# Attention with layer norms and a sign FFN: a step's scores and maxima issued in two rounds of two heads

## The chip, the cores and the metric

The kernel runs on one core of a Trainium2 chip. The metric is the device time of one execution in microseconds (us). Before the change three timed runs gave 4376.77, 4377.27 and 4377.44 us; the median is 4377.27.

The engines are called as the profile calls them: PE is TensorE (PEld its weight loads), ACT is ScalarE, DVE is VectorE, POOL is GpSimd, SP is SyncE. PSUM is the memory that PE writes its results to: eight banks, each 128 partitions by 512 f32 values here.

## The reference

Input x is 4 x 2048 x 512 in f32. There are 16 heads of 32 columns.

```
q, k, v = x @ Wq.T, x @ Wk.T, x @ Wv.T          # split into 16 heads of 32
attn    = softmax(q k^T / sqrt(32)) v            # per batch and head, over 2048 keys
x       = layernorm(x + attn)
w       = +1 or -1 by the sign of the FFN weights
y       = clip((x @ w.T) * scale + bias, -100, 100)
out     = layernorm(x + y)
```

## The kernel before

**Groups, query blocks, steps.** The work is cut into 16 groups n: four batches by four sets of four heads. A group's queries come in four blocks of 512 (qb), its keys in 16 chunks of 128 (kc). One step s is one chunk of keys against one block of queries for the four heads of a group: 64 steps a group, 1024 steps in all. Heads of 32 columns fill a quarter of PE's rows, so head h uses the row strip h (partitions 32h to 32h + 31) and four heads can stand side by side.

**Scores (L325 to L344).** The scores of a step are transposed: 128 keys on the partitions, 512 queries in the columns, one PSUM bank for each head. The softmax needs the row maximum subtracted, so each bank gets two matmuls: at L329 ones times `negm` (the negated maxima, split into three bf16 parts that sum to the f32 value) starts the accumulation, and at L335 key times query in f32 is added. Four bf16 matmuls are issued, then four f32 ones. ACT then takes the exponential of each bank (L342) into `p`, which has five buffers.

**Maxima (L266 to L303).** Before a block's scores can start, its maxima must be known. They are found by a second score matmul in the other orientation (queries on the partitions), 22 steps ahead: `units(s)` says which units of maxima step s computes. One unit is 128 queries against 512 keys for four heads: four f32 matmuls (L277) into four banks. DVE finds the maxima of the first three heads from PSUM (L284). The fourth bank is copied by ACT to a tile `moved` in SBUF (L296), and the function `later` has DVE search that tile near the end of the step. `max_parts` (L305) joins a block's parts, splits them into bf16 and issues the transposing DMA that makes `negm`; in one step of each block it stands between the first and the second maximum on DVE.

**The rest of a step.** In the order of issue (loop at L843): scores, maxima, then "fillers" that a planner (L770) has chosen, such as projections for the next group (`piece`, L235), transposes, FFN thirds or denominators. In every even step follows `weighted` (L346): the probabilities of the two steps before times v, on column strips, into one bank, which DVE adds to an SBUF tile (L365). Then `later`, and `add_up` (L374): POOL adds `p` to the running sum of the block (L379), 14 of 16 steps in a block.

**What sets the order.** The schedule is manual: each engine executes in the order of issue. Which PSUM bank is used is decided at build time by `take` (L82): it picks the bank that a small clock model (`runs`, `spend`, `give`) thinks is free first. The model decides nothing but the bank. On the chip a matmul waits by semaphore until its bank has been read.

```
def give(i, engine, us):
    free_at[i] = spend(engine, us, clock["PE"] + 0.2) + 0.1
```

Of the kernel before, what the change touches and what calls it, by code (L numbers as in the profile page):

```python
# [11 lines left out]
F32 = mybir.dt.float32  # L12
BF16 = mybir.dt.bfloat16
AF = mybir.ActivationFunctionType
ALU = mybir.AluOpType
AX = mybir.AxisListType
# [4 lines left out]
def kernel(  # L21
# [11 lines left out]
    nc = tc.nc  # L33
    B, S, D = x.shape
    P = 128
    H = 16
    HD = D // H
    HG = 4
    NG = H // HG
    DC = D // P  # L40
    QB = 512
    NQB = S // QB
    NTQ = QB // P
    NT = S // P
    NKB = S // QB
    EPS = 1e-5
    MAX_VAL = 100.0
    SM_SCALE = 1.0 / math.sqrt(HD)
    STEPS = NQB * NT
# [7 lines left out]
    const = ctx.enter_context(tc.tile_pool(name="const", bufs=1))  # L57
    xpool = ctx.enter_context(tc.tile_pool(name="xpool", bufs=2))
    stage = ctx.enter_context(tc.tile_pool(name="stage", bufs=2))
    mpool = ctx.enter_context(tc.tile_pool(name="mpool", bufs=2))  # L60
    cpool = ctx.enter_context(tc.tile_pool(name="cpool", bufs=1))
    dram = ctx.enter_context(tc.tile_pool(name="dram", bufs=1, space=bass.MemoryType.DRAM))
    xtpool = ctx.enter_context(tc.tile_pool(name="xtpool", bufs=NQB))
# [3 lines left out]
    ppool = ctx.enter_context(tc.tile_pool(name="ppool", bufs=5))  # L67
# [3 lines left out]
    small = ctx.enter_context(tc.tile_pool(name="small", bufs=2))  # L71
# [5 lines left out]
    ps = psum.tile([P, 8, QB], F32, name="ps")  # L77
    clock = {"PE": 0.0, "ACT": 0.0, "DVE": 0.0}
# [3 lines left out]
    def take():  # L82
        i = min(range(8), key=lambda k: free_at[k])
        clock["PE"] = max(clock["PE"], free_at[i])
        free_at[i] = math.inf
        return i

    def runs(shape, us):

        clock["PE"] += us + (0.1 if form[0] != shape else 0.0)  # L90
        form[0] = shape

    def spend(engine, us, ready=0.0):
        clock[engine] = max(clock[engine], ready) + us
        return clock[engine]

    def give(i, engine, us):

        free_at[i] = spend(engine, us, clock["PE"] + 0.2) + 0.1

    def cols_of(i, a, b):
        return ps[:, i, : a * b].rearrange("p (a b) -> p a b", a=a)
# [4 lines left out]
    ones_bf = const.tile([P, P], BF16, name="ones_bf")  # L107
# [81 lines left out]
    xc = {}  # L189
    kT = {}  # L190
    qT = {}
    vv = {}
    negm = {}
    parts = {}
# [68 lines left out]
        piece(tokens(n, t), weights("wv", n), vv[n][:, t, :], P)  # L263


    def max_unit(n, qb, u, between):  # L266

        qc, kb = divmod(u, NKB)
        if u == 0:
            parts[n, qb] = small.tile([P, NTQ, HG, NKB], F32, tag="part", name="part")  # L270
        part = parts[n, qb]
        if n == qb == 0:
            kb, qc = divmod(u, NTQ)
        banks = [take() for _ in range(HG)]
        for h in range(HG):
            rows = slice(h * HD, (h + 1) * HD)
            nc.tensor.matmul(  # L277
                ps[:, banks[h], :], lhsT=qT[n, qb][rows, ts(qc, P)],
                rhs=kT[n][rows, ts(kb, QB)], start=True, stop=True,
            )  # L280
        runs("rows", 0.86)

        def row_max(h, src):
            nc.vector.tensor_reduce(  # L284
                part[:, qc, h : h + 1, kb], src, AX.X, ALU.max, negate=True
            )

        for h in range(HG - 1):
            row_max(h, ps[:, banks[h], :])
            give(banks[h], "DVE", 0.6)  # L290
            if h == 0 and between is not None:
                max_parts(*between, banks[h])
                give(banks[h], "DVE", 1.25)

        moved = mpool.tile([P, QB], F32, tag="moved", name="moved")
        nc.scalar.copy(moved, ps[:, banks[-1], :])  # L296
        give(banks[-1], "ACT", 0.6)

        def later():
            row_max(HG - 1, moved)  # L300
            spend("DVE", 0.6, clock["ACT"])

        return later  # L303

    def max_parts(n, qb, i):  # L305
        part = parts.pop((n, qb))
        nm = cols_of(i, NTQ, HG)
        sp = split[qb % 2]
        nc.vector.tensor_reduce(nm, part, AX.X, ALU.min)
        nc.vector.tensor_copy(sp[:, :, :, 0], nm)  # L310
        nc.vector.tensor_tensor(nm, nm, sp[:, :, :, 0], ALU.subtract)
        nc.vector.tensor_copy(sp[:, :, :, 1], nm)
        nc.vector.tensor_tensor(sp[:, :, :, 2], nm, sp[:, :, :, 1], ALU.subtract)
        negm[n, qb] = small.tile([P, QB], BF16, tag="negm", name="negm")
        nc.sync.dma_start_transpose(
            out=negm[n, qb].rearrange("p (t q) -> p t q", t=NTQ),
            in_=sp.rearrange("p t h d -> p (t h d)"),
        )
# [3 lines left out]
    def is_last(n, qb):  # L322
        return n == B * NG - 1 and qb == NQB - 1

    def scores(n, qb, kc):  # L325
        banks = [take() for _ in range(HG)]
        for h in range(HG):
            rows = slice(h * HD, (h + 1) * HD)
            nc.tensor.matmul(  # L329
                ps[:, banks[h], :], lhsT=ones_bf[rows, :], rhs=negm[n, qb][rows, :],  # L330
                start=True, stop=False,
            )
        for h in range(HG):
            rows = slice(h * HD, (h + 1) * HD)
            nc.tensor.matmul(  # L335
                ps[:, banks[h], :], lhsT=kT[n][rows, ts(kc, P)], rhs=qT[n, qb][rows, :],
                start=False, stop=True,
            )
        runs("rows", 1.08)
        p = ppool.tile([P, HG, QB], F32, tag="p", name="p")  # L340
        for h in range(HG):
            nc.scalar.activation(p[:, h, :], ps[:, banks[h], :], AF.Exp, scale=SM_SCALE)  # L342
            give(banks[h], "ACT", 0.49)
        return p  # L344

    def weighted(pair):  # L346
# [36 lines left out]
    def ones_times(b, p, start, stop):  # L383
        for h in range(HG):
            nc.tensor.matmul(  # L385
                ps[h * HD : (h + 1) * HD, b, :], lhsT=ones, rhs=p[:, h, :],
                start=start, stop=stop,
            )
        runs("cols", 0.86)
# [12 lines left out]
    def denominators(n, qb):  # L402

        if is_last(n, qb):
            b = sums[0]
        else:
            b = take()
            for k, p in enumerate(last_p.pop((n, qb))):
                ones_times(b, p, k == 0, False)
            whole = acc.pop((n, qb))  # L410
            ones_times(b, whole, False, True)
        if is_last(n, qb):
            dT = mpool.tile([P, QB], F32, tag="moved", name="dT")
        else:
            dT = whole[:, 0, :]
        nc.scalar.copy(dT, ps[:, b, :])
        give(b, "ACT", 0.6)
        acc[n, qb] = dT
        if not is_last(n, qb):
            columns_of_sums(n, qb)  # L420
            at(step[0] + 2, reciprocals, n, qb)
# [184 lines left out]
    ahead = {}  # L606
# [3 lines left out]
    def at(step, f, *args):  # L610
        behind[step].append(lambda: f(*args))
# [78 lines left out]
    start = -LEAD0 - 5  # L690
# [66 lines left out]
    def units(s):  # L757

        def first(s):
            return min(max(s + min(LEAD0 + max(s, 0) // 2, LEAD), 0), total)  # L760

        return range(first(s), first(s + 1))
# [74 lines left out]
    _, used = plan()  # L837
    chosen, _ = plan(used)
    held = []
    before = None  # L840
    s = start
    step = [start]
    while s <= max(*chosen, *behind):  # L843
        step[0] = s
        now = None
        if 0 <= s < total:
            n, at_n = divmod(s, STEPS)
            qb, kc = divmod(at_n, NT)
            now = (n, qb, kc, scores(n, qb, kc))
        fillers = chosen[s]  # L850
        if s < 0:
            for t in fillers:
                t[3](*t[4])
        later, more = None, list(units(s))
        if more:
            n, at_n = divmod(more.pop(0), STEPS)
            later = max_unit(n, *divmod(at_n, NT), ahead.get(s))
        elif s in ahead:
            i = take()
            max_parts(*ahead[s], i)  # L860
            give(i, "DVE", 1.25)
        if s == total:
            weighted(held)
            held = []
        if s >= 0:
            for t in fillers:
                t[3](*t[4])
        if s % 2 == 0 and held:
            weighted(held)
            held = []  # L870
        if later is not None:
            later()
        for u in more:
            n, at_n = divmod(u, STEPS)
            max_unit(n, *divmod(at_n, NT), None)()
        if now is not None:
            add_up(*now, before)
            before = now[3]
            held.append(now)
        for f in behind[s]:  # L880
            f()
        s += 1
# [36 lines left out]
```

## Time and profile before

| | before |
|---|---|
| median of three runs | 4377.27 us |
| span of the profiled execution | 4375.3 us, about 2 us below the timed runs |
| first score matmul starts | 70.5 us |
| last add on POOL ends | 4302.6 us |
| PE clock granted | 0.997 of full |
| ACT exponentials (L342) | 4096 x 602 ns, 2114.8 us busy |
| DVE weighted sums (L365) | 448 x 692 ns |
| POOL running sums (L379) | 889 adds of about 4.54 us |
| DMA | 101.4 MB, mean 23 GB/s |

The span is from the first to the last instruction of one profiled execution. A group line of the profile has line, engine, operation, output and inputs, shape and count; behind the bar stand the busy time in us, the mean of one in ns, and the idle time just ahead of them with what ended most of it. An f32 matmul appears as two rows, each with its weight load, so four heads make eight rows. In a timeline each line has start, length, engine, line, operation and count. Lengths of PE rows are modelled and contain some time of the pipeline, so starts are compared.

### The profile page before, as it was taken

How to read it: one execution, taken by the hardware profiler on the slowest of the kernel's cores; microseconds unless marked ns; L12 is line 12 of the kernel's file. 1: busy time of each engine (PE TensorE's matmuls, PEld its weight loads, DVE VectorE, ACT ScalarE, POOL GpSimd, SP SyncE). 2: the span in 40 equal slices, each digit the busy share in tenths (PEclk: the TensorE clock that was granted, in tenths of full speed). 3: DMA queues.
4: the chain of work that ended last, by engine and by line, in shares of the span. 5: the costliest groups of instructions: out<-in, count | busy, mean ns of one | idle time of the engine just before them, and what ended most of it. 6: DMA issues, size and time to landing. Idle time of an engine off the chain costs nothing.

```text
span 4375.3 us, 89213 instructions
## 1 busy us (share of the span) xinstructions
PE 4340.7 (99%) x36092; PEld 2136.2 (49%) x36092; DVE 3316.3 (76%) x5908; ACT 2998.5 (69%) x6173; POOL 4082.7 (93%) x940
## 2 busy tenths in 40 slices
PE   9999999999999999999999999999999999999998
PEld 5444444454454554445445454455545544455443
DVE  6777777777777777777777777777777777777774
ACT  4666666676667667676676766767667676767665
POOL 4999999999999999999999999999999999999993
PEclk9999999999999999999999999999999999999999
DMA  2000000010001000011000100001100000001101
GB/s 72 11 13 17 11 21 10 16 40 18 21 13 29 11 23 20 11 45 36 21 20 11 33 10 21 23 10 50 28 20 21 20 21 23 20 11 33 24 23 49
DMA packets 260326, 101.40 MB, mean 23 GB/s; under 512 B 169420, under 2 KB 234956, under 8 KB 259912
## 3 DMA queue, kind: packets, MB, share of 16 engines
q1 hardware_dynamic: 258952, 93.86, 8.9%
q8 instruction: 282, 4.62, 0.4%
q10 hardware_dynamic: 960, 1.84, 0.1%
q14 instruction: 132, 1.08, 0.1%
HBM read 54.26 MB, written 33.02 MB: 20 GB/s over the span
## 4 chain that ended last, share of the span: by engine, by line
PE 95%; POOL 2%; ACT 1%; DVE 1%; issue 0%; DMA 0%; ACTq 0%; POOLq 0%; DVEq 0%; SPq 0%
PE ps L353 21%; PE ps L277 20%; PE ps L335 20%; PE ps L235 16%; PE ps L329 8%; PE ps L568 5%; PE ps L385 3%; POOL acc L379 2%; PE ps L427 1%; PE ps L223 1%; PE ps L554 1%; ACT p L342 1%; DVE part L284 1%; ACT xg_last L544 0%; PE ps L135 0%
## 5 line engine op out<-in xcount | busy, mean ns | idle before, releaser
L379 POOL TENSOR_TENSOR acc<-acc,p 128x2048 f32<-128x2048 f32 x825 | 3743.3, 4537 | 102.6 <-ACT p L342 42.4
L342 ACT ACTIVATE p<-ps 128x512 f32<-128x512 f32 x4096 | 2114.8, 602 | 1130.9 <-PE ps L335 1124.8
L284 DVE TENSOR_REDUCE part<-ps 128x1 f32<-128x512 f32 x3072 | 1934.0, 683 | 771.2 <-PE ps L277 770.8
L277 PE MATMUL ps<-kT,qT 32*128 32x512 f32 x8192 | 1112.2, 590 | 0.1
L335 PE MATMUL ps<-qT,kT 32*128 32x512 f32 x8192 | 1075.8, 592 | 0.0
L353 PE MATMUL ps<-p,vv 128*32 128x512 f32 x8192 | 983.4, 598 | 0.2 <-ACT p L342 0.2
L277 PEld LDWEIGHTS ps<-kT,qT 32*128 32x128 f32 x8192 | 541.4, 185 | 379.5 <-issue 189.4
L284 DVE TENSOR_REDUCE part<-moved 128x1 f32<-128x512 f32 x1024 | 692.4, 676 | 0.5 <-ACT moved L296 0.4
L296 ACT COPY moved<-ps 128x512 f32<-128x512 f32 x1024 | 631.1, 616 | 20.2 <-PE ps L277 19.6
L353 PEld LDWEIGHTS ps<-p,vv 128*32 128x32 f32 x8192 | 220.1, 109 | 685.7 <-issue 345.1
L329 PE MATMUL ps<-negm,ones_bf 32*128 32x512 bf16 x4096 | 442.5, 385 | 8.6 <-DMA negm<-split 3.9
L335 PEld LDWEIGHTS ps<-qT,kT 32*128 32x128 f32 x8192 | 407.4, 185 | 44.4 <-issue 27.4
L379 POOL TENSOR_TENSOR acc<-p 128x2048 f32<-128x2048 f32 x64 | 290.8, 4544 | 103.9 <-ACT p L342 103.9
L365 DVE TENSOR_TENSOR oT<-ps,oT 128x512 f32<-128x512 f32 x448 | 309.8, 692 | 94.3 <-PE ps L353 57.7
L329 PEld LDWEIGHTS <-ones_bf 32*128 32x128 bf16 x4096 | 105.8, 91 | 554.9 <-issue 521.6
L235 PEld LDWEIGHTS ps<-wvT,xT 128*128 128x128 f32 x2048 | 251.1, 191 | 79.6 <-ACT p L342 74.0
L235 PE MATMUL ps<-wvT,xT 128*128 128x128 f32 x2048 | 279.3, 280 | 0.3 <-ACT p L342 0.2
L235 PE MATMUL ps<-xT,wqT 128*128 128x256 f32 x1024 | 250.2, 387 | 0.0
L235 PE MATMUL ps<-xT,wkT 128*128 128x256 f32 x1024 | 249.1, 387 | 0.0
L235 PEld LDWEIGHTS ps<-xT,wkT 128*128 128x128 f32 x1024 | 184.8, 189 | 65.4 <-ACT p L342 43.2
L235 PEld LDWEIGHTS ps<-xT,wqT 128*128 128x128 f32 x1024 | 184.3, 189 | 61.9 <-ACT p L342 41.0
L568 PEld LDWEIGHTS ps<-wsT,nT 128*128 128x128 f32 x1152 | 167.8, 189 | 94.3 <-ACT p L342 93.3
(75 smaller groups left out, 1720.3 us busy)
## 6 DMA issues: line engine op xcount, KB each, us to landing
xc<-in_L_attn_x_dram SPq DMA_DIRECT2D x60, 256.0 KB
res<-xc SPq DMA_DIRECT2D x60, 256.0 KB
xs<-in_L_attn_x_dram SPq DMA_DIRECT2D x48, 256.0 KB
xg<-res SPq DMA_DIRECT2D x12, 1024.0 KB
out_dram<-xg SPq DMA_DIRECT2D x12, 1024.0 KB
first_x<-in_L_attn_x_dram SPq DMA_DIRECT2D x16, 256.0 KB
xg_last<-res SPq DMA_DIRECT2D x4, 768.0 KB
out_dram<-xg_last SPq DMA_DIRECT2D x3, 1024.0 KB
```

The lines of the kernel that those rows point to most:

```text
L235: nc.tensor.matmul(pp, lhsT=lhs(c), rhs=rhs(c), start=(c == 0), stop=(c == DC - 1))
L277: nc.tensor.matmul(ps[:, banks[h], :], lhsT=qT[n, qb][rows, ts(qc, P)], rhs=kT[n][rows, ts(kb, QB)], start=True, stop=True,)
L284: nc.vector.tensor_reduce(part[:, qc, h : h + 1, kb], src, AX.X, ALU.max, negate=True)
L296: nc.scalar.copy(moved, ps[:, banks[-1], :])
L329: nc.tensor.matmul(ps[:, banks[h], :], lhsT=ones_bf[rows, :], rhs=negm[n, qb][rows, :], start=True, stop=False,)
L335: nc.tensor.matmul(ps[:, banks[h], :], lhsT=kT[n][rows, ts(kc, P)], rhs=qT[n, qb][rows, :], start=False, stop=True,)
L342: nc.scalar.activation(p[:, h, :], ps[:, banks[h], :], AF.Exp, scale=SM_SCALE)
L353: nc.tensor.matmul(pb[cols, :], lhsT=vv[n][:, kc, cols], rhs=p[:, h, :], start=(i == 0), stop=(i == 1),)
L365: nc.vector.tensor_tensor(outs[n, qb], pb, outs[n, qb], ALU.add)
L379: nc.gpsimd.tensor_tensor(a, before if kc == 1 else a, p, ALU.add)
L385: nc.tensor.matmul(ps[h * HD : (h + 1) * HD, b, :], lhsT=ones, rhs=p[:, h, :], start=start, stop=stop,)
L568: nc.tensor.matmul(py, lhsT=self.nT[j][:, c, :], rhs=wT["ws"][:, c, cols], start=(c == 0), stop=(c == DC - 1),)
```

## The change

`scores` and `max_unit` become one function, `scores_and_maxima`, that works in two rounds. In round one heads 0 and 1 score while heads 2 and 3 are searched for maxima; in round two heads 2 and 3 score and heads 0 and 1 are searched. A round takes four banks and issues: the two bf16 matmuls, the two maxima matmuls, the two f32 score matmuls, then two exponentials on ACT and two maxima on DVE. All four maxima are read from PSUM. The copy at L296, the tile `moved`, its pool and `later` go. `max_parts` now follows head 0's maximum in round two, the third of the step. Steps without scores or without maxima leave out those parts and keep the two rounds. The small tile `dT` of the last block moves to another pool. The clock model is told 0.97 us for a round with scores and 0.43 for one without.

```diff
-    def max_unit(n, qb, u, between):
...
-        for h in range(HG - 1):
-            row_max(h, ps[:, banks[h], :])
-            give(banks[h], "DVE", 0.6)
...
-        moved = mpool.tile([P, QB], F32, tag="moved", name="moved")
-        nc.scalar.copy(moved, ps[:, banks[-1], :])
-        give(banks[-1], "ACT", 0.6)
...
-    def scores(n, qb, kc):
...
+    def scores_and_maxima(score, u, between):
+
+        low, high = range(HG // 2), range(HG // 2, HG)
...
+        for scored, searched in ((low, high), (high, low)):
+            scored = scored if score is not None else ()
+            searched = searched if u is not None else ()
+            banks = {h: take() for h in (*scored, *searched)}
+            for h in scored:
+                nc.tensor.matmul(
+                    ps[:, banks[h], :], lhsT=ones_bf[strip(h), :], rhs=negm[n, qb][strip(h), :],
+                    start=True, stop=False,
+                )
+            for h in searched:
+                nc.tensor.matmul(
+                    ps[:, banks[h], :], lhsT=qT[mn, mqb][strip(h), ts(qc, P)],
+                    rhs=kT[mn][strip(h), ts(kb, QB)], start=True, stop=True,
+                )
+            for h in scored:
+                nc.tensor.matmul(
+                    ps[:, banks[h], :], lhsT=kT[n][strip(h), ts(kc, P)],
+                    rhs=qT[n, qb][strip(h), :], start=False, stop=True,
+                )
+            runs("rows", 0.97 if scored else 0.43)
+            for h in scored:
+                nc.scalar.activation(p[:, h, :], ps[:, banks[h], :], AF.Exp, scale=SM_SCALE)
+                give(banks[h], "ACT", 0.49)
+            for h in searched:
+                nc.vector.tensor_reduce(
+                    parts[mn, mqb][:, qc, h : h + 1, kb], ps[:, banks[h], :],
+                    AX.X, ALU.max, negate=True,
+                )
+                give(banks[h], "DVE", 0.6)
+                if h == 0 and between is not None:
+                    max_parts(*between, banks[h])
+                    give(banks[h], "DVE", 1.25)
```

More of the change, by code (lines that the diff above doesn't have):

```diff
@@ L59 @@
     stage = ctx.enter_context(tc.tile_pool(name="stage", bufs=2))
-    mpool = ctx.enter_context(tc.tile_pool(name="mpool", bufs=2))
     cpool = ctx.enter_context(tc.tile_pool(name="cpool", bufs=1))
@@ L263, in project_v @@
         piece(tokens(n, t), weights("wv", n), vv[n][:, t, :], P)
-    def max_unit(n, qb, u, between):
[L268 to L286, printed above, removed]
-        for h in range(HG - 1):
-            row_max(h, ps[:, banks[h], :])
-            give(banks[h], "DVE", 0.6)
-            if h == 0 and between is not None:
-                max_parts(*between, banks[h])
-                give(banks[h], "DVE", 1.25)
-        moved = mpool.tile([P, QB], F32, tag="moved", name="moved")
-        nc.scalar.copy(moved, ps[:, banks[-1], :])
-        give(banks[-1], "ACT", 0.6)
[L299 to L303, printed above, removed]
     def max_parts(n, qb, i):
@@ L323, in is_last, with strip @@
         return n == B * NG - 1 and qb == NQB - 1
-    def scores(n, qb, kc):
[L326 to L343, printed above, removed]
+    def strip(h):
+        return slice(h * HD, (h + 1) * HD)
@@ new lines, in unit @@
+    def unit(u):
+        n, at_n = divmod(u, STEPS)
+        qb, at_qb = divmod(at_n, NT)
+        qc, kb = divmod(at_qb, NKB)
+        if n == qb == 0:
+            kb, qc = divmod(at_qb, NTQ)
+        if at_qb == 0:
+            parts[n, qb] = small.tile([P, NTQ, HG, NKB], F32, tag="part", name="part")
+        return n, qb, qc, kb
+    def scores_and_maxima(score, u, between):
+        low, high = range(HG // 2), range(HG // 2, HG)
+        p = None
+        if score is not None:
+            n, qb, kc = score
+            p = ppool.tile([P, HG, QB], F32, tag="p", name="p")
+        if u is not None:
+            mn, mqb, qc, kb = unit(u)
+        for scored, searched in ((low, high), (high, low)):
[30 more added lines that the diff above has]
+                    give(banks[h], "DVE", 1.25)
@@ L412, in denominators @@
         if is_last(n, qb):
-            dT = mpool.tile([P, QB], F32, tag="moved", name="dT")
+            dT = cpool.tile([P, QB], F32, tag="xc", name="dT")
         else:
@@ L844 @@
         step[0] = s
-        now = None
+        now = score = u = None
         if 0 <= s < total:
             n, at_n = divmod(s, STEPS)
-            qb, kc = divmod(at_n, NT)
-            now = (n, qb, kc, scores(n, qb, kc))
+            score = n, *divmod(at_n, NT)
         fillers = chosen[s]
@@ L853 @@
                 t[3](*t[4])
-        later, more = None, list(units(s))
+        more = list(units(s))
         if more:
-            n, at_n = divmod(more.pop(0), STEPS)
-            later = max_unit(n, *divmod(at_n, NT), ahead.get(s))
+            u = more.pop(0)
         elif s in ahead:
@@ L861 @@
             give(i, "DVE", 1.25)
+        if score is not None or u is not None:
+            p = scores_and_maxima(score, u, ahead.get(s) if u is not None else None)
+            if score is not None:
+                now = *score, p
         if s == total:
@@ L870 @@
             held = []
-        if later is not None:
-            later()
         for u in more:
-            n, at_n = divmod(u, STEPS)
-            max_unit(n, *divmod(at_n, NT), None)()
+            scores_and_maxima(None, u, None)
         if now is not None:
```

## Prediction

> **What bounds the kernel now.** I read the page first, from the shares of the engines down to the chain of work and the costliest groups.
>
> ```profile
> span 4375.3 us, 89213 instructions
> ...
> PE 4340.7 (99%) x36092; PEld 2136.2 (49%) x36092; DVE 3316.3 (76%) x5908; ACT 2998.5 (69%) x6173; POOL 4082.7 (93%) x940
> ...
> PE 95%; POOL 2%; ACT 1%; DVE 1%; issue 0%; DMA 0%; ACTq 0%; POOLq 0%; DVEq 0%; SPq 0%
> ...
> L284 DVE TENSOR_REDUCE part<-ps 128x1 f32<-128x512 f32 x3072 | 1934.0, 683 | 771.2 <-PE ps L277 770.8
> ...
> L284 DVE TENSOR_REDUCE part<-moved 128x1 f32<-128x512 f32 x1024 | 692.4, 676 | 0.5 <-ACT moved L296 0.4
> L296 ACT COPY moved<-ps 128x512 f32<-128x512 f32 x1024 | 631.1, 616 | 20.2 <-PE ps L277 19.6
> ```
>
> The reader should see that TensorE (PE) holds 95% of the chain, that ACT and DVE are idle for a quarter to a third of the span, and that POOL, at 93%, is the next bound. The copy at L296, which the change removes, lies on an engine that waits for others.
>
> Next, one ordinary even step in the timeline, PE alone (start, length, line):
>
> ```profile
> 2002.95 0.40 PE L329 MATMUL ps<-negm,ones_bf 32*128 32x512 bf16 x4
> 2003.18 1.03 PE L335 MATMUL ps<-qT,kT 32*128 32x512 f32 x8
> 2004.04 1.03 PE L277 MATMUL ps<-kT,qT 32*128 32x512 f32 x8
> 2004.99 1.93 PE L353 MATMUL ps<-p,vv 128*32 128x512 f32 x16
> 2006.85 0.39 PE L329 MATMUL ps<-negm,ones_bf 32*128 32x512 bf16 x4
> ```
>
> Starts tell more than lengths, because ends are modelled. Four heads sit on four strips of 32 rows and run side by side: the four bf16 matmuls take 0.23 us (2002.95 to 2003.18), and the f32 ones, which appear as two passes each, take 0.86 for four heads (2003.18 to 2004.04), so 0.43 a pass. Then the maxima's matmuls, 0.86 again, and 0.09 to change to column tiles. So the stage with row strips is 0.23 + 0.86 + 0.86 = 1.95 us, and **each strip is busy for all of it**. Row by row, 1.95 is also the median over the steps.
>
> **What the change does to a strip.** Per strip the matmuls stay what they were: one bf16, two f32. Only their order differs. Strips 0 and 1 keep bf16, score, maxima: 1.95. Strips 2 and 3 now begin the stage with an f32 matmul. The trace has such starts: in the lead-in, maxima follow full-array work directly, with no bf16 matmul ahead. First the maxima's matmuls between 20 and 41 us by shape, then those of the step above (count, busy us, mean ns):
>
> ```profile
> L277 PE MATMUL ps<-kT,qT 32*128 32x512 f32 x52 | 7.6, 644 | 0.0
> ```
> ```profile
> L277 PE MATMUL ps<-kT,qT 32*128 32x512 f32 x8 | 1.0, 587 | 0.0
> ```
>
> In the lead-in first passes last 692 ns and second passes 587; in all 20 places where these matmuls come first after full-array work the second pass of a strip starts 533 ns after its first, against 429 elsewhere. So **an f32 weight load that nothing precedes in its tiling is exposed, for 105 ns**. The bf16 load in the same place costs 13 (384 ns, against 371 where it was preloaded). Today the bf16 matmuls hide the scores' f32 load, and they stand first in all strips.
>
> After: strips 2 and 3 take 0.533 + 0.429 (maxima) + 0.215 (bf16, load hidden) + 0.86 (scores) = 2.04 us. The stage ends with its latest strip, so it grows from 1.95 to 2.04, and with the few ns of stagger between heads I take **0.095 us a step**. Bounds: 0 if the load is pulled ahead of the tiling change; 0.21 if the second round's loads were exposed as well, one more load of 105 behind the first.
>
> The Trainium skill speaks for the lower end: "TensorE: Matmul & The Clock Gate" (Step-by-step: what each phase is for) says that the queue pulls a weight load ahead of matmuls in flight when it aims at the background weight buffer. By that rule this term is 0 and the time falls. The 533 ns in 20 of 20 places disagree, and the measurement decides.
>
> 18 units of maxima run before the first score (144 matmul rows of L277 before 69.9 us, 8 to a unit); four early steps carry two units, so 1024 - 18 - 4 = 1002 steps have the new order. The last 22 steps have scores alone and begin with bf16 in every strip: no cost.
>
> **Does mixing cost anything else?** In 100 or so steps today the fourth bf16 matmul is 100 to 320 ns late and runs beside the other heads' f32 passes; both keep their rate, apart from the 105 of a load that came late. And passes of different strips don't wait for each other's order: where the fourth head lacked a bank, the first three heads ran both passes before it. So I cost the mixing at 0.
>
> **What the removed copy and the new order give back.** ACT loses 1024 copies (631 us busy), DVE reads the fourth maximum from PSUM for 683 ns instead of 676 (+7 us busy, hidden in its idle time). None of that is on PE's path, except through PSUM banks. Row by row I added what the row stages take beyond 1.95: 85 us in the whole span. The pattern is a light odd step with one value piece:
>
> ```profile
> 563.66 0.69 PE L329 MATMUL ps<-negm,ones_bf 32*128 32x512 bf16 x4
> 563.99 1.23 PE L335 MATMUL ps<-qT,kT 32*128 32x512 f32 x8
> 564.95 1.12 PE L277 MATMUL ps<-kT,qT 32*128 32x512 f32 x8
> ```
>
> Here the fourth bf16 matmul waits 0.32 us for the bank of the step before's fourth exponential. After the change round one wants only two score banks and two maxima banks, and DVE begins its maxima a microsecond earlier, so banks freed at about 1.85, 2.35, 2.45 and 2.85 us into a light step of 3.1 are enough: this stall goes. What is late next: round two, which wants four banks 0.96 into the step, the last of them the weighted sum's, freed by DVE. In the step shown that add began 4.11 us after the step's start and took 0.69; 4.8 is 0.9 into the next step. The last matmul of round two wants it by about 1.08, its load 0.1 sooner: it fits by tens of ns, as today.
>
> Where the 85 us lie: 5 in the first 16 steps (start-up, kept), 2.5 up to 420 us, 18 in the 192 steps up to about 1.15 ms, 34 from there to the last 64 steps, 25 in those. The 18 and the new cost there (192 x 0.095 = 18) cancel, and POOL holds that stretch anyway, as busy times by stage show (length, then PE, PEld, DVE, ACT, POOL):
>
> ```profile
> 420.00:1130.00 710.00, 706.21 (x5956) 332.88 (x5954) 528.56 (x888) 489.45 (x1004) 698.78 (x155) 1.00 0.09 20
> 1130.00:4040.00 2910.00, 2909.42 (x24532) 1445.83 (x24531) 2263.87 (x4070) 2027.85 (x4178) 2787.93 (x634) 1.00 0.09 22
> ```
>
> POOL is 98% busy in the first and 96% in the second: PE sets the pace of the second. I let the 34 and 2.5 go, and 12 of the last 25, where odd steps of 2.04 us are no longer than ACT's four exponentials (2.06) and some wait stays.
>
> **Sum**, on the profiled execution: new load 810 steps x 0.095 = +77; stalls -34 - 2.5 - 12 = -49; net +28. Span 4375.3 + 28 = 4403. The timed median is 4377.27, 2.0 above the span, so **4405 us**, 0.6% slower.
>
> **Rivals.**
> 1. *The load is hidden* (ends on the other side). The 105 ns vanish and the stalls go: 4377 - 49 - some 5 = about 4322. POOL can't allow much more: 889 adds of 4.54 us plus 0.08 between them are 4104, with 38 small operations some 4140, against 4223 from first add to last, so at most about 85 us can go. For it: every engine but PE has more room. Against: 20 starts of 20. It decides if the first passes of strips 2 and 3 show 587.
> 2. *Break-even*: the stalls go wholly, also the 25 and some waits for POOL: 4377 + 95 - 85 - 5 = about 4382. For it: the removed copy is ACT work in just the short last steps.
> 3. *Nothing is given back*: bank waits return in round two, since a late bank there now blocks two heads' scores behind it as well. 4377 + 95 = 4472, or more; it decides if matmuls of round two start over 1.1 us into the step. Against: banks come free earlier on both engines.
> 4. *Order binds*: if a score in strip 0 had to let the second pass of strips 2 and 3 begin first, each step would lose 0.3 us, and the time be about 4680. Against it stand the rows of blocked heads above. The same page of the Trainium skill (Part 3, The mechanism) says that matmuls start strictly in program order. By that, two passes a head would serialise the heads and a step cost about 2 us more, some 6400 in all; the 0.86 us for four heads of two passes each disagree.
>
> **Numbers.** Forecast (4386 to 4440) 0.52; rival 1 0.16; rival 2 0.16; rival 3 0.12; rival 4 0.04. So slower by over 0.2% 0.68, within 0.2% (about what a measurement of this kernel can tell from no change) 0.16, faster 0.16. The range 4340 to 4460 leaves out most of rival 1 and of rivals 3 and 4.
>
> **What would show it.** Right: half of the maxima's first passes at 692 ns (a group mean near 613, against 590 now), half of the bf16 ones at 371; column tiles 2.13 us after a step's first matmul (2.04 now); light steps without the 0.3 us wait; ACT near 2370 us busy, POOL's share down a little. Wrong: passes of strips 2 and 3 at 587 from the start; waits of round two on DVE; a score of strip 0 that begins only when the maxima of strips 2 and 3 are done.

## The result, and the profile after

| | before | after |
|---|---|---|
| median of the timed runs | 4377.08 us | 4420.33 us |
| ratio to before, 95% interval | | 1.0098 (1.0087 to 1.0110) |
| span of the profiled execution | 4375.3 us | 4417.3 us |
| first score matmul | 70.5 us | 73.1 us |
| median length of a stage with row strips | 1.951 us | 2.045 us |
| waits in these stages above the median, steps with all parts | 67 us | 21 us |

A row stage is the stretch of a step from its first matmul on row strips to the end of its last; a wait in it is what it takes beyond the median. The lead-in is the time before the first score. A light step has one short filler.

The change made the kernel 1.0% slower, 43 us, where 28 were forecast. From the page of the changed kernel:

```profile
span 4417.3 us, 88158 instructions
...
PE 4381.2 (99%) x36092; PEld 2321.4 (53%) x36092; DVE 3331.3 (75%) x5908; ACT 2513.3 (57%) x5149; POOL 4078.9 (92%) x940
...
PE 95%; POOL 2%; DVE 1%; ACT 1%; issue 0%; DMA 0%; ACTq 0%; POOLq 0%; DVEq 0%; SPq 0%
...
L332 DVE TENSOR_REDUCE part<-ps 128x1 f32<-128x512 f32 x4096 | 2543.8, 682 | 604.3 <-PE ps L318 567.7
```

ACT lost the 1024 copies and 485 us of work, DVE is busy 15 us longer, and the time did not follow either of them: PE still holds 95% of the chain. The same even step as the prediction showed, PE alone:

```profile
2024.94 0.39 PE L313 MATMUL ps<-negm,ones_bf 32*128 32x512 bf16 x2
2024.95 0.70 PE L318 MATMUL ps<-kT,qT 32*128 32x512 f32 x2
2025.17 0.59 PE L323 MATMUL ps<-qT,kT 32*128 32x512 f32 x2
2025.48 0.59 PE L318 MATMUL ps<-kT,qT 32*128 32x512 f32 x2
2025.60 0.59 PE L323 MATMUL ps<-qT,kT 32*128 32x512 f32 x2
2025.91 0.38 PE L313 MATMUL ps<-negm,ones_bf 32*128 32x512 bf16 x2
2026.03 0.59 PE L318 MATMUL ps<-kT,qT 32*128 32x512 f32 x2
2026.13 0.59 PE L323 MATMUL ps<-qT,kT 32*128 32x512 f32 x2
2026.46 0.59 PE L318 MATMUL ps<-kT,qT 32*128 32x512 f32 x2
2026.56 0.59 PE L323 MATMUL ps<-qT,kT 32*128 32x512 f32 x2
2027.08 1.92 PE L349 MATMUL ps<-p,vv 128*32 128x512 f32 x16
```

Read it by strips. Strips 0 and 1: bf16 at 24.94, scores at 25.17 and 25.60, maxima at 26.03 and 26.46. Strips 2 and 3: maxima at 24.95, but their second pass only at 25.48, 0.53 later, while every other pass takes 0.43; then bf16 at 25.91, scores at 26.13 and 26.56. The first maxima pass lasts 0.70, the others 0.59: that is the exposed weight load. Strips 2 and 3 end 0.1 us after strips 0 and 1, and column work begins 2.14 us after the first matmul, against 2.04 before. By shape, in the same step:

```profile
L318 PE MATMUL ps<-kT,qT 32*128 32x512 f32 x8 | 2.1, 613 | 0.0
```

613 ns is (692 + 3 x 587) / 4, as forecast. The step behind a light one shows what the change gave back. After a single value piece (L234) the next step begins without a wait: bf16 at 572.75, scores at 572.97, as in any step.

```profile
571.66 1.16 PE L234 MATMUL ps<-wvT,xT 128*128 128x128 f32 x8
572.75 0.39 PE L313 MATMUL ps<-negm,ones_bf 32*128 32x512 bf16 x2
572.75 0.70 PE L318 MATMUL ps<-kT,qT 32*128 32x512 f32 x2
572.97 0.59 PE L323 MATMUL ps<-qT,kT 32*128 32x512 f32 x2
```

**Where the 42 us of span went**, step by step against before: the lead-in is 2.6 us longer; the row stages 46 us longer in sum (85 more in 822 steps, 39 less in some 170 where a wait went); everything else is about 6 us shorter.

### The profile page after: what moved, and what is told of

The parts are those of the page before. It is cut to its first block, busy times and chain, and to the rows that moved or that the text cites. A ratio compares the mean times of both kernels' runs of the same rounds, so it can differ in the third digit from the quotient of the medians.

```text
span 4417.3 us, 88158 instructions
## 1 busy us (share of the span) xinstructions
PE 4381.2 (99%) x36092; PEld 2321.4 (53%) x36092; DVE 3331.3 (75%) x5908; ACT 2513.3 (57%) x5149; POOL 4078.9 (92%) x940
## 4 chain that ended last, share of the span: by engine, by line
PE 95%; POOL 2%; DVE 1%; ACT 1%; issue 0%; DMA 0%; ACTq 0%; POOLq 0%; DVEq 0%; SPq 0%
PE ps L318 29%; PE ps L349 21%; PE ps L234 16%; PE ps L323 10%; PE ps L313 9%; PE ps L564 5%; PE ps L381 3%; POOL acc L375 2%; PE ps L423 1%; PE ps L222 1%; PE ps L550 1%; DVE part L332 0%; ACT p L329 0%; DVE st L514 0%; ACT xg_last L540 0%
## 5 line engine op out<-in xcount | busy, mean ns | idle before, releaser
L332 DVE TENSOR_REDUCE part<-ps 128x1 f32<-128x512 f32 x4096 | 2543.8, 682 | 604.3 <-PE ps L318 567.7
L318 PE MATMUL ps<-kT,qT 32*128 32x512 f32 x8192 | 2153.1, 616 | 5.3 <-DVE part L332 1.1
L323 PE MATMUL ps<-qT,kT 32*128 32x512 f32 x8192 | 2023.9, 590 | 0.0
L318 PEld LDWEIGHTS ps<-kT,qT 32*128 32x128 f32 x8192 | 779.8, 184 | 107.9 <-issue 11.4
L323 PEld LDWEIGHTS ps<-qT,kT 32*128 32x128 f32 x8192 | 767.3, 184 | 56.5 <-issue 7.1
L313 PE MATMUL ps<-negm,ones_bf 32*128 32x512 bf16 x4096 | 784.8, 380 | 5.0 <-DMA negm<-split 2.9
L313 PEld LDWEIGHTS <-ones_bf 32*128 32x128 bf16 x4096 | 198.0, 92 | 673.8 <-issue 521.0
L234 PEld LDWEIGHTS ps<-wvT,xT 128*128 128x128 f32 x2048 | 251.6, 192 | 79.8 <-ACT p L329 74.6
L234 PE MATMUL ps<-wvT,xT 128*128 128x128 f32 x2048 | 279.3, 280 | 0.0
L234 PE MATMUL ps<-xT,wqT 128*128 128x256 f32 x1024 | 247.7, 385 | 0.0
L234 PE MATMUL ps<-xT,wkT 128*128 128x256 f32 x1024 | 246.6, 385 | 0.1
L234 PEld LDWEIGHTS ps<-xT,wkT 128*128 128x128 f32 x1024 | 185.0, 190 | 64.4 <-ACT p L329 43.4
L234 PEld LDWEIGHTS ps<-xT,wqT 128*128 128x128 f32 x1024 | 184.6, 190 | 60.8 <-ACT p L329 41.0
L564 PE MATMUL ps<-wsT,nT 128*128 128x172 f32 (+1 forms) x1152 | 201.7, 319 | 0.1
L238 ACT COPY vv<-ps 128x128 f32<-128x128 f32 x256 | 69.6, 272 | 147.8 <-PE ps L234 147.6
```

The costliest lines, as they stand in the source:

```text
L234: nc.tensor.matmul(pp, lhsT=lhs(c), rhs=rhs(c), start=(c == 0), stop=(c == DC - 1))
L238: nc.scalar.copy(dst, pp)
L313: nc.tensor.matmul(ps[:, banks[h], :], lhsT=ones_bf[strip(h), :], rhs=negm[n, qb][strip(h), :], start=True, stop=False,)
L318: nc.tensor.matmul(ps[:, banks[h], :], lhsT=qT[mn, mqb][strip(h), ts(qc, P)], rhs=kT[mn][strip(h), ts(kb, QB)], start=True, stop=True,)
L323: nc.tensor.matmul(ps[:, banks[h], :], lhsT=kT[n][strip(h), ts(kc, P)], rhs=qT[n, qb][strip(h), :], start=False, stop=True,)
L332: nc.vector.tensor_reduce(parts[mn, mqb][:, qc, h : h + 1, kb], ps[:, banks[h], :], AX.X, ALU.max, negate=True,)
```

## The experiments

Each kernel ran beside the kernel before; medians of that one lie between 4377.2 and 4377.9 us in these comparisons. Stage lengths and waits are added up row by row from the traces.

**All bf16 matmuls first.** The rounds stay, but strips 2 and 3 also begin with bf16.

```diff
+            if scored and scored[0] == 0:
+                held_banks = {h: take() for h in range(HG)}
...
-            for h in scored:
+            for h in held_banks if scored and scored[0] == 0 else ():
                 nc.tensor.matmul(
-                    ps[:, banks[h], :], lhsT=ones_bf[strip(h), :], rhs=negm[n, qb][strip(h), :],
+                    ps[:, held_banks[h], :], lhsT=ones_bf[strip(h), :], rhs=negm[n, qb][strip(h), :],
```

> The changed kernel, but all four bf16 matmuls of a step are issued first, in round one, so that strips 2 and 3 also begin with bf16 and their f32 load is hidden; the rounds, the reading from PSUM and the removed copy stay. Theory (exposed load): the row stage falls from 2.045 to 1.95 us, first passes of the maxima are 587 ns, and the time is 4420 - 94 = about 4326, less than both kernels; with a few more bank waits, since six banks are wanted at once, up to 4350. Rival (mixing scores and maxima in one round costs the time, whatever begins): stays near 4420.

Measured: 4406.16 us, ratio 1.0067 (1.0051 to 1.0082). The median stage is 1.951 us again, so the load was the 94 ns. The time fell by 14 us instead of 94, for two reasons. The waits are back at 70 us; six banks are now wanted at a step's start, which I take for the reason, though no run isolates it. And something new follows the stage (PE, its end):

```profile
2024.37 0.59 PE L327 MATMUL ps<-qT,kT 32*128 32x512 f32 x2
2024.79 0.59 PE L322 MATMUL ps<-kT,qT 32*128 32x512 f32 x2
2024.80 0.59 PE L327 MATMUL ps<-qT,kT 32*128 32x512 f32 x2
2025.36 0.33 PE L222 MATMUL ps<-ident,xs 128*128 128x128 f32 x1
```

The last passes start at 2024.80, stream for 0.43 and end at 2025.23; full-array work starts 0.13 later, where both kernels need 0.09. It is so in some 760 steps of this run, about 30 us in all. My expectation of 4326 (4350 at most) fell, and the rival's 4420 is not reached either; the ground of mine, the load, stands by the stage.

**Scores ahead of maxima in round two of that run**, to see whether the order of issue makes the 0.13.

```diff
-            for h in searched:
-                nc.tensor.matmul(
...
+            if 0 not in searched:
+                search()
             for h in scored:
                 nc.tensor.matmul(
...
+            if 0 in searched:
+                search()
```

> The run with all bf16 matmuls first, in which round two issues its scores ahead of its maxima. That run's row stage of 1.951 us was followed by 131 ns until column or full-array work began, against 91 in both kernels, which cost some 36 us. Theory A (what is issued last decides the change of tiling): 91 ns again and 4406 - 36 = about 4370. Theory B (maxima and scores that end within 10 ns of each other cost the 40 ns, whatever the order): 131 ns and 4406.

Measured: 4405.93 us, ratio 1.0064 (1.0049 to 1.0079), and again about 130 ns. Theory A is out. In both runs the 40 ns come in 741 of some 776 stages whose last maxima and last score passes start within 12 ns of each other, and in 21 of some 215 others; why is open.

**Maxima first in all strips**, no rounds, copy kept: the kernel before with the two halves of a step exchanged.

```diff
-            now = (n, qb, kc, scores(n, qb, kc))
+            now = (n, qb, kc)
...
             later = max_unit(n, *divmod(at_n, NT), ahead.get(s))
...
+        if now is not None:
+            now = (*now, scores(*now))
```

> The kernel before with its order inside a step turned round: the maxima of all four heads are issued ahead of the scores, no rounds, the copy on ACT stays. Theory (exposed load): every strip now begins with f32, the row stage is 2.045 us, the maxima's first passes are 692 ns in all four strips, and the time is 4377 + 1002 x 0.094 = 4471 less what bank waits change (some tens either way). Rival (the rounds or the mixing cost the time): the row stage stays 1.95 and the time near 4377.

Measured: 4475.13 us, ratio 1.0224 (1.0209 to 1.0239); median stage 2.055 us. One step, PE:

```profile
2005.85 1.14 PE L277 MATMUL ps<-kT,qT 32*128 32x512 f32 x8
2006.82 0.39 PE L329 MATMUL ps<-negm,ones_bf 32*128 32x512 bf16 x4
2007.03 1.04 PE L335 MATMUL ps<-qT,kT 32*128 32x512 f32 x8
2008.00 1.92 PE L353 MATMUL ps<-p,vv 128*32 128x512 f32 x16
```

The same matmuls in another order, without rounds or mixing: 0.97 us to the bf16 matmuls (two passes of 0.43 and the load), and column work 2.15 us after the start. The median stage is 104 ns longer than in the kernel before, the 105 of one exposed load. Some waits went, so the row stages are 89 us longer in sum and the time 98 us. The load alone costs this, without the change's rounds; that settles the main cost.

**The load covered by work**: two useless bf16 matmuls of 256 columns a step ahead of the maxima in strips 2 and 3; the maxima overwrite their result.

```diff
             for h in searched:
+                if h in high and scored:
+                    nc.tensor.matmul(
+                        ps[:, banks[h], :W], lhsT=ones_bf[strip(h), :],
+                        rhs=negm[n, qb][strip(h), :W], start=True, stop=True,
+                    )
```

> The changed kernel with two useless bf16 matmuls of 256 columns a step, on strips 2 and 3 ahead of their maxima in round one, into banks that the maxima then overwrite. Theory (what costs 94 ns is the f32 weight load, not the strip's work): the 107 ns of added streaming hide the load, first passes of these maxima fall from 692 to 587 ns, the row stage stays within 20 ns of 2.045 us and the time within 25 us of 4420. Rival (the strips' work sets the stage and the load is not what is late): each step grows by 0.107 us or more, and the time is about 4530.

Measured: 4438.86 us, ratio 1.0140 (1.0125 to 1.0155), 18.5 us over the changed kernel for 2004 matmuls more. Three groups of matmul rows between 2000 and 2100 us, by shape:

```profile
L323 PE MATMUL ps<-kT,qT 32*128 32x512 f32 x176 | 43.8, 589 | 0.0
...
L313 PE MATMUL ps<-negm,ones_bf 32*128 32x512 bf16 x88 | 17.0, 380 | 0.0
...
L319 PE MATMUL ps<-negm,ones_bf 32*128 32x256 bf16 x44 | 6.3, 278 | 0.0
```

The maxima's mean is 589 instead of 613: no load of theirs is exposed. The 107 ns of streaming cost 18 ns a step in the time and 24 in the median stage (2.069 us, where I had allowed 20), since they run in the time of the load. What a strip lost is a load without anything ahead of it.

**The rounds with the copy**: head 1's maximum, the last of a step, goes through ACT and SBUF as the fourth did before.

```diff
+                if h == 1:
+                    moved = mpool.tile([P, QB], F32, tag="moved", name="moved")
+                    nc.scalar.copy(moved, ps[:, banks[h], :])
...
+                    later.append(lambda: nc.vector.tensor_reduce(
+                        at_1, moved, AX.X, ALU.max, negate=True))
```

> The changed kernel with the copy put back: head 1's maximum (the last of the step) goes through ACT and an SBUF tile as the fourth did before. Theory: the row stage stays 2.045 us; what the removed copy gave back in bank waits is lost again, so 4420 to 4450. Rival (the copy's removal is what costs, DVE's fourth PSUM read being late): under 4410.

Measured: 4422.83 us, ratio 1.0104 (1.0087 to 1.0121); median stage 2.045 us and waits 23 us, as without the copy. The time is 2.5 us above the changed kernel, which the intervals don't tell apart. So in rounds no worth of the copy shows, and its removal is not what gave the waits back. That part of my theory fell.

**No copy and no rounds**: four heads score, then four are searched, DVE reads all from PSUM.

```diff
-        for scored, searched in ((low, high), (high, low)):
+        for scored, searched in ((range(HG), ()), ((), range(HG))):
...
-            runs("rows", 0.97 if scored else 0.43)
+            if scored or searched:
+                runs("rows", 1.08 if scored else 0.86)
```

The clock model is told the times of the kernel before again.

> The changed kernel with the rounds undone: all four heads score, then all four are searched, as before; the copy on ACT stays gone and DVE reads every maximum from PSUM. Theory (exposed load costs, early banks give back, the copy's removal by itself is worth little): the row stage is 1.95 us again, the bank waits are at least those of before (67 us over the median stage), since the fourth maxima bank is now freed by DVE later than the copy freed it: 4375 to 4400. Rival (the removed copy is what gave the waits back): waits stay near the 21 us of the changed kernel, and the time is 4377 - 45 = about 4330.

Measured: 4529.2 us, ratio 1.0346 (1.0329 to 1.0363), the slowest of all: against the kernel before, the copy's removal costs 151 us. That includes whatever the model's choice of banks changed with it, which no run separates. I expected 4400 at most. The row stages of the 1024 steps are 154 us longer in sum: 63 in odd steps, 91 in even ones. DVE in an even step and the step behind it, in the kernel before and here:

```profile
2005.09 1.89 DVE L284 TENSOR_REDUCE part<-ps 128x1 f32<-128x512 f32 x3 [1.00 <-PE ps L277]
2007.06 0.69 DVE L365 TENSOR_TENSOR oT<-ps,oT 128x512 f32<-128x512 f32 x1
2007.67 0.67 DVE L284 TENSOR_REDUCE part<-moved 128x1 f32<-128x512 f32 x1
```
```profile
2044.99 2.48 DVE L333 TENSOR_REDUCE part<-ps 128x1 f32<-128x512 f32 x4 [1.59 <-PE ps L318]
2047.39 0.68 DVE L362 TENSOR_TENSOR oT<-ps,oT 128x512 f32<-128x512 f32 x1
```

Before, three maxima end in time and the weighted sum is added 1.97 us after the first of them began; the fourth maximum follows, since it waits in SBUF. Here four maxima stand ahead of the add, which starts 2.40 us after the first. The bank that the add frees is the last one that the next step's maxima need: their last weight load starts at 2048.13, 0.05 us after the add's end. PE in that next, odd step:

```profile
2046.75 0.39 PE L313 MATMUL ps<-negm,ones_bf 32*128 32x512 bf16 x4
2046.98 1.02 PE L323 MATMUL ps<-qT,kT 32*128 32x512 f32 x8
2047.84 1.41 PE L318 MATMUL ps<-kT,qT 32*128 32x512 f32 x8
2049.18 0.66 PE L222 MATMUL ps<-ident,xs 128*128 128x128 f32 x4
```

The maxima's eight passes span 1.41 us instead of 1.02, and full-array work starts 2.43 us after the step's start. Such waits make up the 63 us of the odd steps. The 91 lie in even steps, behind steps without a weighted sum. There the last bank is one that DVE leaves later because it now reads the fourth maximum from PSUM too: the bank of that maximum itself (some 36 us), or that of an attention or FFN sum queued behind it (some 54). An even step behind a light one, with DVE ahead of it:

```profile
719.20 2.49 DVE L333 TENSOR_REDUCE part<-ps 128x1 f32<-128x512 f32 x4 [1.16 <-PE ps L318]
```
```profile
721.48 1.38 PE L318 MATMUL ps<-kT,qT 32*128 32x512 f32 x8
```
```profile
721.74 0.29 PEld L318 LDWEIGHTS ps<-kT,qT 32*128 32x128 f32 x2
```

The fourth maximum ends at 721.69, and the last maxima load starts 0.05 us later. So the copy at L296 was not idle ACT filling: it freed its own bank, and it let DVE free others in time. In rounds DVE starts its first two maxima a microsecond earlier (1.17 us after the step's start instead of 2.14), and all four are done before the weighted sum; DVE in the changed kernel's step of above:

```profile
2026.11 2.48 DVE L332 TENSOR_REDUCE part<-ps 128x1 f32<-128x512 f32 x4 [1.08 <-PE ps L318]
2029.14 0.69 DVE L361 TENSOR_TENSOR oT<-ps,oT 128x512 f32<-128x512 f32 x1 [0.55 <-PE ps L349]
```

The add now waits for PE and not for maxima, and the copy is not needed.

**max_parts behind the first maximum of its step** (in rounds, head 2's).

```diff
-                if h == 0 and between is not None:
+                if h == HG // 2 and between is not None:
```

> The changed kernel with max_parts moved on DVE from behind the third maximum of its step to behind the first, where it stood before. Theory: it matters only in the lead-in, where the first block's maxima are awaited: the first score starts 1.2 us earlier (two maxima of 0.6 us), about 71.9 instead of 73.1 us; the time falls by 1 to 2 us, and by no more than 5. Rival (max_parts in mid-step delays banks in all 64 blocks): 10 us or more.

Measured: 4419.55 us, ratio 1.0095 (1.0080 to 1.0110), 0.8 us under the changed kernel, which the intervals don't tell apart. The first score starts at 72.35 us, 0.76 earlier instead of 1.2. The rival (10 us) is out; the 1.2 is not shown, since kernels with the same lead-in differ by 0.6 us there.

**Rounds only behind light steps.** All steps as before with the copy, rounds only in the even step behind an odd one with one short filler. In a second kernel behind any single filler.

```diff
+    def after_light(s):
+        f = chosen[s - 1] if s - 1 in chosen else []
+        return 1 < s < total and s % 2 == 0 and len(f) == 1
...
```

The first kernel also asks that the filler is no wide projection.

> The order of before with its copy in nearly all steps; the two rounds only in an even step that follows an odd step whose one filler is short (a value piece, an FFN third, a transpose). In before 87 of 88 steps that follow a single value piece wait for a bank, 25 us in all, and the other short fillers add some 15. Theory (rounds pay 94 ns a step and save the waits that a light step leaves): some 110 steps x 0.094 = 10 us paid, some 30 to 35 us of waits saved, so 4377 - 20 to 25 = 4352 to 4357, faster than both kernels. Rival (rounds take as much elsewhere as they give): 4370 to 4390.

> As the run with rounds after light steps, but also after odd steps whose single filler is a wide projection (104 steps, of which 40 wait in before, 14 us in all). Theory: 104 x 0.094 = 10 us more paid, 14 saved at best: within 6 us of the other run.

Measured: 4385.85 us, ratio 1.0019 (1.0010 to 1.0028), and 4392.01 us, 1.0034 (1.0021 to 1.0046), where 4352 to 4357 was forecast. Hardly any wait went: in the first kernel 96 stages are longer by 12 us in sum and 8 shorter by 1.5. The load came on top. The step behind a value piece in the first of them:

```profile
572.01 1.16 PE L235 MATMUL ps<-wvT,xT 128*128 128x128 f32 x8
573.10 0.39 PE L316 MATMUL ps<-negm,ones_bf 32*128 32x512 bf16 x2
573.11 1.01 PE L321 MATMUL ps<-kT,qT 32*128 32x512 f32 x2
573.43 0.70 PE L326 MATMUL ps<-qT,kT 32*128 32x512 f32 x2
```

Scores start 0.33 us after the bf16 matmuls instead of 0.22: one of the two maxima of round one lacked its bank, and the scores, issued behind it, waited with it. I had put the cure in the step that waits; the banks come from the step before it.

**Rounds in the light step itself**, and in a second kernel in any odd step with a single filler.

```diff
-    def after_light(s):
+    def light(s):
-        f = chosen[s - 1] if s - 1 in chosen else []
-        return 1 < s < total and s % 2 == 0 and len(f) == 1
+        f = chosen[s]
+        return 0 < s < total and s % 2 == 1 and len(f) == 1
...
```

Here too the first kernel asks that the filler is no wide projection.

> As the run with rounds after light steps, but the rounds stand in the light odd step itself (one short filler), not in the step behind it. The last run showed that the step behind one waits all the same, since the banks it wants are those that the light step frees; in rounds the light step's own first two maxima are searched a microsecond earlier. Theory: the light steps pay 0.094 us each (some 110, 10 us), the waits of the steps behind them (some 35 us in before) go: 4377 - 20 to 25 = 4352 to 4357, faster than both kernels. Rival (the waits are not cured by early maxima): 4385 or more.

> As the run with rounds in light steps, also in odd steps with one wide projection (104 steps; 14 us of waits behind them in before). Theory: 10 us more paid, up to 14 saved: within 6 us of the other run.

Measured: 4365.65 us, ratio 0.9973 (0.9963 to 0.9983), and **4360.27 us, 0.9961 (0.9948 to 0.9975): faster than both kernels**. The first misses its forecast of 4352 to 4357 by 9 us. The stages did what was forecast, 10 us paid and 32 saved; but in the 192 steps where I let POOL hold the pace they are 7 us shorter in sum and the time is not, which is most of the miss. In the second, 207 stages are longer by 20 us in sum (97 ns each) and 144 shorter by 45. A light step of it ends at 562.32, and the next starts without a wait:

```profile
561.23 1.16 PE L235 MATMUL ps<-wvT,xT 128*128 128x128 f32 x8
562.32 0.40 PE L316 MATMUL ps<-negm,ones_bf 32*128 32x512 bf16 x4
562.54 1.03 PE L326 MATMUL ps<-qT,kT 32*128 32x512 f32 x8
563.40 1.03 PE L321 MATMUL ps<-kT,qT 32*128 32x512 f32 x8
```

So rounds pay where a wait of some 0.3 us stands behind enough of them; in every step, as in the changed kernel, they lose. The chain of work of the second shows who is next:

```profile
PE 93%; POOL 5%; ACT 1%; DVE 1%; issue 0%; DMA 0%; ACTq 0%; POOLq 0%; DVEq 0%; SPq 0%
```

## Why the prediction was right, point by point

- **PE bounds, and a strip's work is unchanged: right.** PE holds 95% of the chain in both kernels, and 485 us less work on ACT bought nothing by itself. (My 2370 us for ACT took off all 631 us of the copies and came out at 2513: rows of ACT overlap, as the four exponentials of 602 ns in 2.06 us show.)
- **An f32 load that nothing precedes in its tiling costs 105 ns, and the stage grows by 0.095 us: right** (1.951 to 2.045, so 0.094). Maxima first shows it without rounds, bf16 first takes it away, the covered load fills it with work. The rule of the Trainium skill in "TensorE: Matmul & The Clock Gate" (Step-by-step: what each phase is for), by which the load would have been pulled ahead, did not hold across this change of tiling in any of these runs. Rival 1 is out. So is rival 3: round two starts 0.97 us into the step shown, not over 1.1.
- **Mixing costs nothing: right for the passes**, which keep 0.43 us, and for their order (rival 4): scores of strips 0 and 1 begin at 2025.17 while the second maxima pass of strips 2 and 3 starts at 2025.48. A matmul that lacks its bank does hold the ones issued behind it, in other strips too (573.43 above). And two of my runs paid 40 ns at the stage's end where maxima and scores end together; in the changed kernel they end 0.1 us apart and pay nothing.
- **Waits given back: too many were let go in the sum.** The row stages grew by 46 us instead of the load's 1002 x 0.094 = 94, so 48 came back. That this is close to the 49 of the sum is luck: 14 of the 48 lie in the stretch where POOL leads, which the sum left out. Elsewhere 34 came back instead of 49. In the middle 24 of 34 us of waits went instead of all, and 8 of 12 at the end.
- **The cause of it was half wrong.** I gave it to the removed copy and the new order together; the rounds with the copy show that the order does it all, and the run without copy and rounds that the removal by itself costs 151 us. The step that failed is the cost of DVE's fourth read of PSUM, "+7 us busy, hidden in its idle time": I counted DVE's busy time, not the place in its queue, and so not the banks that it frees later. In rounds this costs nothing, since DVE starts earlier; that saved the forecast. I had named the weighted sum's bank as what is late next, with tens of ns to spare, and did not see that the copy guards that bank among others.
- **What was mis-sized: the sum, 28 us instead of 42.** The largest miss is the 15 us of waits that stayed; what lies outside the row stages became about 6 us shorter, which I had not forecast, and hides part of it. By stretches, measured against forecast: lead-in 2.6 against 0; first 16 steps 1.9 against 1.5; up to step 79 4.3 against 3.6; the 192 steps where I let POOL hold the pace 2.0 against 0; the long middle 36.1 against 31; the last 64 steps -4.8 against -8. The largest single term that I left out is the lead-in. There DVE sets the pace, its maxima followed each other at 0.62 us instead of 0.60, and max_parts stands behind two more of them; I had costed that edit at nothing without naming it.

DVE's lead-in in the changed kernel, 43 maxima in 26.76 us:

```profile
42.38 26.76 DVE L332 TENSOR_REDUCE part<-ps 128x1 f32<-128x512 f32 x43 [0.91 <-PE ps L318]
```

How the 2.6 us divide among pace, place and the start of DVE's work (0.47 us later than before) is not settled: with max_parts moved the first score came 0.76 us earlier, but it also differs by 0.6 (72.9 to 73.5 us) among runs whose lead-in is that of the changed kernel.

## What to carry to other kernels

Where PE is full, an edit that leaves its work the same can still lose by what stands first after a change of tiling: put a matmul there whose load is cheap, as the bf16 one here, in every strip that is used, and check what the new order costs: here that gave back the 94 ns of the stage but only 14 us of the time. A copy on an idle engine is not free to remove: ask what is pushed back in the queue of the engine that takes its work, and which buffers come free later by it. And a cure for a wait belongs where the buffer is freed late, not where it is missed; applied only there, its price is paid only there.

## What the runs showed of the hardware that I had not expected

- Row-strip stages whose maxima and scores end within some 10 ns of each other are followed by 131 ns until column or full-array work (741 of some 776 such stages in each of two runs), against a median of 90 to 91 in all other runs. Which of the two is issued last does not change it; no run here shows the cause.
- The second pass of an f32 matmul in one strip does not hold matmuls issued behind it in other strips (scores at 2025.17, second maxima pass at 2025.48), but a matmul that waits for its bank does (573.43). Weight loads did not cross the change of tiling in any of these runs; that costs 105 ns for 128 f32 columns and 13 ns for bf16.
- 107 ns of bf16 streaming in two strips cost 18 ns a step (24 in the median stage) where it ran in the time of an f32 load.
